# A two-layer graph network in one launch: earlier loads, later moments, denser products for the first group, and one copy moved from VectorE to ScalarE

## The chip, the cores and the metric

The kernel runs on one core of a Trainium2 chip, in float32 throughout. The metric is device time in microseconds (us) of one execution; lower is better. Engines are called PE (TensorE), DVE (VectorE), ACT (ScalarE), POOL (GpSimd) and SP (SyncE, which only issues DMAs here).

## What is computed

There are 64 graphs of 256 nodes with 256 features: `x` is 64 x 256 x 256 and `adj` has the same shape. Two layers follow, each with a normalization ahead of it and its input added back at the end:

```python
h = maximum(layernorm(x), 0)
A = adj + I;  d = rowsum(A) ** -0.5
x = x + relu((d A d) @ h @ W.T + b)               # layer 0
h = maximum(layernorm(x), 0)                       # layer 1 from here
conv = relu(bn2(conv17(relu(bn1(conv1(h))))) + h)  # 17 taps along the nodes
s = h @ w_se.T + b_se
msg = exp(-|s_i - s_j|^2) @ relu(h @ w_msg.T + b_msg)
x = x + GRU(input=[conv, msg], state=h)            # r, z, n gates
```

In the kernel the weight exp(...) is multiplied by the adjacency of the graph, transposed, as its mask.

## The kernel before

The work has two stages. **Stage 1** (lines 545 to 1280) walks over the graphs. One turn n of the loop at line 1190 works on several graphs at once, each at another step: `turn_h` of graph n-2, `aggregate` of graph n, `turn_cols` (even n), `turn_adj` of graph n+1, `pass_messages` of graph n-5, `messages` of n-2, `distance` (even n), `project` of n, `conv1` of n-2. After each group of matmuls stands `beat(us)`. **Stage 2** (from line 1282) computes the gates of the GRU for four groups of 16 graphs, and beside each group the convolution of the next one.

**Order of the work.** All instructions of PE, ACT, DVE and POOL keep the program's order (`Pinned`, line 94). Only the DMAs of SP are placed by the scheduler of the language, each as soon as it takes its buffer to be free and in program order among those that are ready; SP then runs them in that order. Follow-up work is put off by `after(k, go)` (line 247), which runs `go` at the (k+1)th beat from there. Within a turn there are nine beats and eight slots, `item()` (line 1154), into which extra work can be put.

**The convolution** with 17 taps is done in the frequency domain for 16 graphs at a time. `filter_part` (line 790) makes the spectra of the taps, in 32 steps. `spectrum` (line 294) transforms one half of a graph: 32 steps for a group, each of four matmuls into a tile `df` and a copy to `Xf` by ACT. `product` (line 328) multiplies one of 24 frequencies: matmuls into `y` and `y1`, a copy `k32` on ACT, two results on DVE (`Xf<-y,k`), one sum `xs` on POOL, three loads `wf` of 256 KB each. The inverse transform (`inverse_three`, `inverse_group`, `inverse_last`, lines 376 to 522) is cut into pieces of one instruction, on DVE, POOL and ACT. It starts when product u = 7 is done, and its last part when product 23 is.

**The planner of these pieces** is `Paced` (line 106). Pieces stand in lines, with a cost each (line 110: on DVE 0.15 us and 0.35 per 256 columns). A beat gives room, `share` times its length (0.31 on DVE, 0.5 on POOL, 0.25 on ACT in stage 1, line 1168), at most 1.0 saved up, and pieces are issued while there is room. `paced.lines` is empty before the inverse starts and after its last piece is issued. `paced.drain()` (line 1523) issues what is left when stage 2 begins.

**Pace of the slots.** For the first group, filter steps take the slots from turn 12 on, spectra from turn 29, then products. The rate is set by `FILTER`, `SPECTRA`, `PRODUCTS` (line 1188):

```python
pace[1] = min(pace[1] + pace[0], 1.0)
if items and pace[1] > 0.999:
    pace[1] -= 1.0
    items.pop(0)()
```

with `pace[0]` at `SPECTRA / 8`, later `PRODUCTS / 8`, and `pace[1]` at -3.0 when the spectra begin.

**Loads and moments of layer 0.** `load(g)` (line 816) brings x and adj of a pair of graphs, 512 KB each, into one of three buffers each. The buffer of x comes free when `rows` in `project` (line 935) has added x to the result; the same step stores that result, `x2d`. `row_moments` (line 832) takes mean and variance of the rows of x on DVE (four pairs of instructions for a pair of graphs), `degrees` (line 844) the row sums of adj, also on DVE; `factors` (line 862) on POOL makes scales of both, and `layer0_in` (line 876) on ACT the normalized input `hs` that `aggregate` reads.

**h2T.** `turn_h` (line 984) transposes the normalized input of layer 1 on PE into a PSUM tile `ht`. Its follow-up `keep` copies it into `h2T` in SBUF by DVE (line 997) and stores it (`hTd`). `messages` and `conv1` of the same turn multiply from h2T. It has two buffers, as have `x2`, `c1o` and `xnT`; h2T is written again when the store of two graphs before has landed.

**PSUM.** The tiles ht, ag, st, at, nm, di (four at once), o, df, y and y1 take turns in five banks, named `ps`.

**The hand-over.** When the loop ends, all pools of stage 1 but those of the convolution are closed and the pool `gates` is opened over their place. In it lie `wiT` and `whT` (weights, loaded at lines 1299 and 1300), `T1` to `T4` (sums of weights, made by POOL) and `xcT` (32 KB of each partition), the convolution's output, which `turn_outputs` (line 524) fills: PE transposes into `yt`, ACT and DVE copy out in turn.

Of the kernel before, what the change touches and what calls it, by code (L numbers as in the profile page):

```python
# [11 lines left out]
FP = mybir.dt.float32  # L12
# [16 lines left out]
OUT = 32  # L29
# [156 lines left out]
def gnn_kernel(  # L186
# [10 lines left out]
    B, N, D = x.shape  # L197
    P = 128
    KW = conv2_w.shape[2]
    NB = N // P  # L200
    DC = D // P
    G = 2
# [42 lines left out]
    paced = Paced(pool, vec, act)  # L245

    def after(beats, go):
        due.append([beats, go])
# [296 lines left out]
    with ExitStack() as one:  # L545
# [270 lines left out]
        def load(g):  # L816

            xt = io.tile([P, NR, D], FP, tag="x", name=f"x_{g}", bufs=3)
            at = io.tile([P, NR, N], FP, tag="adj", name=f"adj_{g}", bufs=3)
            st[g].update(both=(xt, at))  # L820
            for b in range(G):
                rb = slice(b * NB, (b + 1) * NB)
                st[g + b].update(xt=xt[:, rb, :], at=at[:, rb, :])
            if g > 0:
                nc.sync.dma_start(xt, x[g : g + G].rearrange("b (c p) d -> p (b c) d", p=P))
                nc.sync.dma_start(at, adj[g : g + G].rearrange("b (c p) d -> p (b c) d", p=P))
# [5 lines left out]
        def row_moments(g, rows):  # L832
            xt, _ = st[g]["both"]
            if "mv" not in st[g]:
                st[g]["mv"] = small.tile([P, NR, 2], FP, tag="mv0", name=f"mv0_{g}", bufs=1)
            for r in rows:
                s6 = small.tile([P, 6], FP, tag="st", name=f"st0_{g}_{r}")
                vec.bn_stats(s6, xt[:, r, :])
                vec.bn_aggr(st[g]["mv"][:, r, :], s6)
# [36 lines left out]
        def layer0_in(g, rows):  # L876

            xt, _ = st[g]["both"]
            rsd, nmr, dis = st[g]["rsd"], st[g]["nmr0"], st[g]["dis0"]
            if rows[0] == 0:  # L880
                hs = work.tile([P, NR, D], FP, tag="hs", name=f"hs_{g}")
                for b in range(G):
                    rb = slice(b * NB, (b + 1) * NB)
                    st[g + b].update(hs=hs[:, rb, :], dis=dis[:, rb])
            for r in rows:
                act.activation(
                    st[g + r // NB]["hs"][:, r % NB, :], xt[:, r, :], AF.Relu,
                    bias=nmr[:, r : r + 1], scale=rsd[:, r : r + 1],
                )
# [94 lines left out]
        def turn_h(g):  # L984
            s = st[g]
            t = bank(f"ht_{g}").rearrange("p (c i) -> p c i", c=DC)
            for dc in range(DC):
                for nb in range(NB):
                    pe.transpose(
                        t[:, dc, nb * P : (nb + 1) * P],  # L990
                        s["h2"][:, nb, dc * P : (dc + 1) * P],
                        ident,
                    )

            def keep():
                s["hT"] = work.tile([P, DC, N], FP, tag="h2T", name=f"h2T_{g}")
                vec.tensor_copy(s["hT"], t)
                nc.sync.dma_start(hT_d[g].rearrange("p (c n) -> p c n", c=DC), s["hT"])
            after(1, keep)

# [184 lines left out]
            items.append(products)  # L1185
            items.extend(lambda u=u: product(u) for u in range(1, UNITS))

        FILTER, SPECTRA, PRODUCTS = 2, 5, 3
        filtering = []
        for n in range(B + 5):  # L1190
            even, odd = n % G == 0, n % G == 1
            if filtering and not items:
                filtering.clear()
                while due:
                    beat(0.0)
                conv_start()
            if even and n + 2 * G < B:
                after(3, lambda n=n: load(n + 2 * G))
            if 2 <= n <= B + 1:
                turn_h(n - 2)  # L1200
            beat(0.4)
            item()
            if n < B:
                aggregate(n)
                if odd and n + 1 < B and n > 0:
                    after(2, lambda n=n: factors(n + 1))
                    for r in range(NR):
                        after((5, 7, 8, 9)[r], lambda r=r, n=n: layer0_in(n + 1, (r,)))
                if even and n + G < B:
                    after(4, lambda n=n: degrees(n + G))  # L1210
                if odd and n + 3 < B:
                    for r in (0, 2):
                        after(3 + r // 2, lambda r=r, n=n: row_moments(n + 3, (r, r + 1)))
            beat(1.7)
            item()
            if even and 4 <= n <= B + 2:
                turn_cols(n - 4)
            beat(0.2)
            if n + 1 < B:
                turn_adj(n + 1)  # L1220
            beat(0.4)
            item()
            if n >= 5:
                pass_messages(n - 5)
            beat(1.7)
            item(True)
            if 2 <= n <= B + 1:
                messages(n - 2)
            beat(1.7)
            item()  # L1230
            if even and 4 <= n <= B + 2:
                distance(n - 4)
            beat(0.6)
            item()
            if n < B:
                project(n)
            beat(1.7)
            item(True)
            if 2 <= n <= B:
                conv1(n - 2)  # L1240
            elif n == B + 2:
                conv1(B - 1)
            beat(1.7)
            item()
            if n == 0:
                small_turns()
                turn_part(wmT, nat_wm, 0, D, "wm")
                T(WI, 0)()
                L(WI, 4)()
                own_bank("ms", 0, bmB)  # L1250
            if n == 1:
                small_shift()
                turn_part(w1T, nat_w1, 0, D, "w1", scale=sc[:, 0:DC])
                beat(0.4)
                own_bank("c1", 0, b1B)
                T(WI, 2)()
                L(WH, 0)()
            if n >= 2 and later:
                for go in later.pop(0):
                    go()  # L1260
                if not later:
                    while due:
                        beat(0.0)
                    prep_stack.close()
                    spec_stack = ExitStack()
                    spec = spec_stack.enter_context(tc.tile_pool(name="spec", bufs=1))
                    tab = spec.tile([P, 3 * UNITS], FP, tag="tab", name="tab")
                    nc.sync.dma_start(tab, nc.inline_tensor(filter_table(), name="tab_c").ap())
                    tp = {k: filter_load(k) for k in range(2)}
                    filtering.append(True)  # L1270
                    pace[:] = FILTER / 2, -7.0
                    items.extend(
                        lambda k=k, j=j: filter_part(k, j) for k in range(4) for j in range(QC // 8)
                    )
# [19 lines left out]
    cv.beat = beat  # L1294
    cv.bank = lambda name: ps_m.tile([P, 2 * D], FP, tag="m", name=name)

    wiT = big.tile([P, 2 * DC, 3 * D], FP, tag="wiT", name="wiT")
    whT = big.tile([P, DC, 3 * D], FP, tag="whT", name="whT")
    nc.sync.dma_start(whT, wh_d)
# [220 lines left out]
    for q in range(1, GROUPS + 1):  # L1520
        share[:] = 0.6, 0.6, 0.3
        ld = gate_inputs(q - 1, 0)
        paced.drain()
        xcT = big.tile([P, DC, P, OUT], FP, tag="xcT", name=f"xcT_{q}")
        turn_outputs(xcT)
        for go in gate_parts(ld, xcT):
            go()
        todo = []
        if q < GROUPS:
            conv_begin(q)  # L1530
            for g in range(NG):
                if g >= NG - WF:
                    wf_load(g - NG + WF)
                for cb in range(DC):
                    spectrum(g, cb)
            for u in range(1, AHEAD):
                sums(u)
            todo = [lambda u=u: product(u) for u in range(UNITS)]
            for _ in range(LEAD):
                todo.pop(0)()  # L1540
        for g in range(NG):
            share[:] = (0.42, 0.55, 0.3) if todo else (0.51, 0.62, 0.3)
            between = [todo.pop(0) if todo else lambda: None for _ in range(PER)]
            ahead, nxt = None, None
            if g + 1 < NG:
                ahead = gate_inputs(q - 1, g + 1)
                nxt = gate_parts(ahead, xcT)
            gates(ld, between, nxt)
            ld = ahead
            if q + 1 < GROUPS and g >= NG - H1:  # L1550
                h1_load(q + 1, g - NG + H1)
# [34 lines left out]
```

## Time and profile before

| what | value |
|---|---|
| median of three runs | 2088.32 us (2087.17 to 2089.09) |
| the profiled execution | 2086.44 us |
| its span, first to last instruction | 2084.7 us |
| mean granted TensorE clock | 0.993 |
| busy, share of the span | PE 97%, weight load 83%, DVE 68%, ACT 47%, POOL 53% |
| stage 1, and the hand-over to it | 0 to about 848 us, then to 864 us |
| filter steps on PE | 161.8 to 364 us |
| spectra of the first group | until about 485 us |
| products of the first group | 485.7 to about 640 us |
| last transpose ht of stage 1 | 833.81 us |

Nearly all instructions carry line 102, the helper that records them, so groups are told apart by the names of the tiles: `ag<-adjH,hs` is the aggregation, `ms` the messages, `o` the projection, `c` the first convolution, `nm` the message passing. A number in brackets after an instruction is the time its engine stood idle before it, with what ended that. A turn of the loop can be found by its transposes `ht`, of which there is one group a turn from n = 2 on. Turns without slot work take about 9.5 us (odd n) and 10.8 us (even n) on PE; a turn with two filter steps takes 12.3 and 13.6, one with four spectra 12.8 and 14.1.

### The profile page before, as it was taken

How to read it: one execution, taken by the hardware profiler on the slowest of the kernel's cores; microseconds unless marked ns; L12 is line 12 of the kernel's file. 1: busy time of each engine (PE TensorE's matmuls, PEld its weight loads, DVE VectorE, ACT ScalarE, POOL GpSimd, SP SyncE). 2: the span in 40 equal slices, each digit the busy share in tenths (PEclk: the TensorE clock that was granted, in tenths of full speed). 3: DMA queues.
4: the chain of work that ended last, by engine and by line, in shares of the span. 5: the costliest groups of instructions: out<-in, count | busy, mean ns of one | idle time of the engine just before them, and what ended most of it. 6: DMA issues, size and time to landing. Idle time of an engine off the chain costs nothing. (4 is left out here: it accounts for less than half of the span.)

```text
span 2084.7 us, 31178 instructions
## 1 busy us (share of the span) xinstructions
PE 2029.4 (97%) x9977; PEld 1728.8 (83%) x9977; DVE 1413.3 (68%) x3207; ACT 987.4 (47%) x2139; POOL 1101.0 (53%) x1313
## 2 busy tenths in 40 slices
PE   7979999999999999899999999999999999999998
PEld 6867777888888878788888888888888888888887
DVE  6556666544498998426989814989923889965444
ACT  4756666665446666522334432334442234343333
POOL 4333333334675564447767617766725867644343
PEclk9989999999999999999999999999999999999999
DMA  8796888756765644556434356533356524322331
GB/s 306 241 243 224 236 255 271 228 171 205 237 220 193 199 167 147 197 175 214 128 103 128 117 176 197 172 107 122 114 150 203 160 86 127 118 87 90 93 100 61
DMA packets 292458, 352.85 MB, mean 169 GB/s; under 512 B 19492, under 2 KB 232119, under 8 KB 291639
## 3 DMA queue, kind: packets, MB, share of 16 engines
q1 hardware_dynamic: 291680, 346.26, 53.0%
q0 software_dynamic: 288, 4.46, 0.6%
q8 instruction: 80, 1.31, 0.3%
q14 instruction: 84, 0.68, 0.1%
q10 hardware_dynamic: 326, 0.14, 0.0%
HBM read 224.43 MB, written 126.35 MB: 168 GB/s over the span
## 5 line engine op out<-in xcount | busy, mean ns | idle before, releaser
L102 DVE TENSOR_TENSOR Xf<-y,k 128x256 f32<-128x256 f32 x184 | 69.1, 417 | 180.1 <-PE y L102 168.9
L102 DVE SCALAR_TENSOR_TENSOR Xf<-Xf 128x256 f32<-128x256 f32 (+1 forms) x248 | 183.2, 753 | 5.3 <-ACT Xf L102 4.2
L102 PE MATMUL ta<-T,S 128*128 128x256 f32 x768 | 186.6, 379 | 0.0
L102 PE MATMUL y<-wf,Xf 128*128 128x256 f32 x768 | 182.4, 380 | 1.7 <-DVE Xf L102 1.4
L102 POOL TENSOR_TENSOR rz<-u,p 128x256 f32<-128x256 f32 x64 | 47.8, 748 | 245.0 <-ACT u L102 245.0
L102 POOL TENSOR_TENSOR rs<-ve,mhalf 128x2 f32<-128x2 f32 (+1 forms) x65 | 46.9, 722 | 231.5 <-DVE nm L102 226.6
L102 ACT ACTIVATE rz<-rz 128x512 f32<-128x512 f32 x128 | 80.2, 627 | 180.1 <-DVE rz L102 180.1
L102 PEld LDWEIGHTS y<-wf,Xf 128*128 128x128 f32 x768 | 144.3, 190 | 24.5 <-DVE Xf L102 2.6
L102 PEld LDWEIGHTS ta<-T,S 128*128 128x128 f32 x768 | 145.9, 190 | 19.8
L102 PE MATMUL n<-wiT,hx 128*128 128x256 f32 x512 | 152.3, 379 | 0.0
L102 POOL TENSOR_TENSOR aT<-e,adjT 128x512 f32<-128x512 f32 x64 | 85.2, 1349 | 103.1 <-ACT e L102 103.0
L102 POOL TENSOR_TENSOR xs<-Xf 128x256 f32<-128x256 f32 x92 | 70.5, 772 | 130.9 <-ACT Xf L102 65.6
L102 PE MATMUL ag<-adjH,hs 128*128 128x256 f32 x512 | 123.4, 384 | 15.9 <-ACT hs L102 10.8
L102 DVE SCALAR_TENSOR_TENSOR h2l<-rz,h2l 128x256 f32<-128x256 f32 x128 | 102.8, 803 | 53.0 <-POOL h2l L102 53.0
L102 PE MATMUL o<-w0T,aggT 128*128 128x256 f32 x512 | 126.1, 390 | 6.4 <-ACT aggT L102 5.1
L102 PE MATMUL ms<-wmT,h2T 128*128 128x259 f32 x512 | 126.3, 389 | 6.0 <-DVE h2T L102 5.9
L102 PE MATMUL n<-whT,hx 128*128 128x256 f32 x512 | 131.4, 379 | 0.0
L102 PE MATMUL n<-wiT,xcT 128*128 128x256 f32 x512 | 131.4, 379 | 0.0
L102 PEld LDWEIGHTS ms<-wmT,h2T 128*128 128x128 f32 x512 | 95.9, 191 | 34.9 <-issue 13.5
L102 POOL TENSOR_TENSOR adjH<-adjT,eye 128x512 f32<-128x512 f32 x64 | 82.7, 1292 | 79.2 <-ACT adjT L102 79.1
L102 PE MATMUL c<-w1T,h2T 128*128 128x256 f32 x512 | 122.8, 383 | 0.0
L102 PE MATMUL nm<-aT,mso 128*128 128x256 f32 x512 | 121.7, 381 | 0.8 <-POOL aT L102 0.8
(182 smaller groups left out, 5251.9 us busy)
## 6 DMA issues: line engine op xcount, KB each, us to landing
wf<-wfd SPq DMA_DIRECT2D x284, 256.0 KB
wfd<-fo SPq DMA_DIRECT2D x32, 576.0 KB
x2d<-x SPq DMA_DIRECT2D x64, 256.0 KB
h2d<-h SPq DMA_DIRECT2D x64, 256.0 KB
hTd<-h2T SPq DMA_DIRECT2D x64, 256.0 KB
h1d<-c1o SPq DMA_DIRECT2D x64, 256.0 KB
xnd<-xnT SPq DMA_DIRECT2D x64, 256.0 KB
h1l<-h1d SPq DMA_DIRECT2D x64, 256.0 KB
```

The lines of the kernel that those rows point to most:

```text
L102: return self.tc.keep_in_program_order(getattr(self.engine, op)(*args, **kwargs))
```

## The change

Five edits are made together.

```diff
             def keep():
                 s["hT"] = work.tile([P, DC, N], FP, tag="h2T", name=f"h2T_{g}")
-                vec.tensor_copy(s["hT"], t)
+                (act.copy if any(paced.lines) else vec.tensor_copy)(s["hT"], t)
...
-        FILTER, SPECTRA, PRODUCTS = 2, 5, 3
+        FILTER, SPECTRA, PRODUCTS = 2, 7, 4
...
             if even and n + 2 * G < B:
-                after(3, lambda n=n: load(n + 2 * G))
+                load(n + 2 * G)
...
+                if even and 0 < n < B - G:
+                    for r in (0, 2):
+                        after(1 + r // 2, lambda r=r, n=n: row_moments(n + G, (r, r + 1)))
                 if even and n + G < B:
                     after(4, lambda n=n: degrees(n + G))
-                if odd and n + 3 < B:
-                    for r in (0, 2):
-                        after(3 + r // 2, lambda r=r, n=n: row_moments(n + 3, (r, r + 1)))
...
+    def outputs_turned(q):
+        return big.tile([P, DC, P, OUT], FP, tag="xcT", name=f"xcT_{q}")
+
+    xcT = outputs_turned(1)
     wiT = big.tile([P, 2 * DC, 3 * D], FP, tag="wiT", name="wiT")
...
         paced.drain()
-        xcT = big.tile([P, DC, P, OUT], FP, tag="xcT", name=f"xcT_{q}")
+        if q > 1:
+            xcT = outputs_turned(q)
         turn_outputs(xcT)
```

- **The copy h2T** is made by ACT while `paced.lines` holds pieces of an inverse, and by DVE otherwise.
- **SPECTRA** goes from 5 to 7 and **PRODUCTS** from 3 to 4.
- **The load** of a pair is written at the start of an even turn, where it stood three beats later.
- **The moments** of a pair were taken in the odd turn ahead of the even turn that takes its degrees; they are now taken in that even turn, two to three beats after `aggregate` and ahead of `degrees`.
- **xcT** of the first group is the first tile of its pool, so that it lies where `wiT` and `whT` lay, and these behind it. Later groups use the same place.

## The prediction

> **What bounds the kernel now.** I read, in this order, the shares of part 1, busy time by stretch of 25 us, the waits of each stretch, and the timelines of the stretches where TensorE (PE) is not full. Columns of the stretches: length, then busy us and instructions of PE, weight load, DVE, ACT and POOL, then the granted clock, DMA share and GB/s.
>
> ```profile
> 125.00:150.00 25.00, 15.41 (x82) 12.69 (x80) 8.24 (x30) 7.92 (x17) 6.99 (x9) 0.85 0.98 202
> 425.00:450.00 25.00, 25.00 (x133) 21.93 (x132) 11.00 (x37) 16.14 (x35) 7.76 (x10) 1.00 0.52 168
> 700.00:725.00 25.00, 23.09 (x122) 19.16 (x119) 23.57 (x64) 15.94 (x35) 15.58 (x18) 1.00 0.64 208
> 850.00:875.00 25.00, 20.23 (x120) 17.22 (x120) 12.01 (x18) 13.56 (x26) 13.12 (x18) 0.93 0.82 284
> ```
>
> PE is full nearly everywhere (425: 25.00 of 25), so work off PE is free there, and the end moves only where PE waits. Besides the start (10.9 us idle in the first 25) that is three places: one gap at 140, a string of small ones from 700 to 845 with DVE at 23.57 of 25, and the hand-over at 850. After 875 each 25 us has 23.9 to 25 us of PE; nothing there is edited.
>
> The gap at 140: the waits from 125 to 160, then PE, then SP's queue.
>
> ```profile
> DVE st L102 <- DMA x<-in_x_dram: 13.6, 1, 13.6
> PE ag L102 <- ACT hs L102: 10.2, 1, 10.2
> ...
> 150.60 2.93 PE L102 MATMUL ag<-adjH,hs 128*128 128x256 f32 x6 [10.18 <-ACT hs L102]
> 154.17 1.06 PE L102 MATMUL at<-ident,adj 128*128 128x128 f32 x4
> ...
> 131.22 0.39 SPq L945 DMA_DIRECT2D x2d<-x  x1
> 133.63 0.34 SPq L1026 DMA_DIRECT2D h1d<-c1o  x1
> 134.06 0.38 SPq L998 DMA_DIRECT2D hTd<-h2T  x1
> 135.74 0.39 SPq L825 DMA_DIRECT2D x<-in_x_dram  x1
> ```
>
> DVE stands 13.6 us before the moments of a pair whose x was issued at 135.74, behind the ten tp loads (119.5 to 129.3) and three stores. Behind DVE stand cols, behind those ACT's mso, behind that hs, which PE needs. PE then runs at half clock for a while (1.06 us where 0.60 is usual). `ht` to `ht`, this turn (n = 12) takes 139.38 to 164.85 = 25.5 us; turn 28, also even with one filter step, takes 358.58 to 370.75 = 12.2. **The gap costs 13.3 us.**
>
> The string: PE's waits from 640 to 910, and one case on DVE and PE.
>
> ```profile
> PE ms L102 <- DVE h2T L102: 5.9, 5, 2.1
> PE first L102 <- ACT xnT L102: 3.1, 1, 3.1
> PE yt L102 <- ACT xcT L102: 2.4, 1, 2.4
> ...
> 707.50 1.50 DVE L102 TENSOR_TENSOR Xf<-Xf,hr 128x256 f32<-128x256 f32 x1
> 708.92 0.68 DVE L102 COPY h2T<-ht 128x512 f32<-128x512 f32 x1
> ...
> 777.17 3.53 PE L102 MATMUL ms<-wmT,h2T 128*128 128x259 f32 x8 [2.07 <-DVE h2T L102]
> ```
>
> The largest item is h2T, late behind the inverse's pieces on DVE. The 2.07 us wait also dropped the clock (3.53 us for 1.9). The string's h2T part: 5.9 + 1.6 = 7.5 us.
>
> The hand-over:
>
> ```profile
> 850.94 0.56 ACT L102 COPY xnT<-nm 128x512 f32<-128x512 f32 x1
> 857.19 0.33 SPq L1299 DMA_DIRECT2D whT<-whd  x1
> 857.36 0.75 DVE L102 TENSOR_SCALAR xcT<-yt,sh 128x512 f32<-128x512 f32 x1 [3.20 <-DMA xnd<-xnT]
> ```
>
> PE ends the last nm at 848.44; its copy xnT comes at 850.94, since ACT waits 2.10 us for the inverse's last pieces; xnd is issued at 853.68; when it lands, at about 857.1 (3.4 us), the first xcT and whT start together. PE reaches the next spectra at 864.26.
>
> [...] the same 128x256 pieces take 0.42 us alone and 1.5 to 2.2 beside POOL. [...] The trace: 0.68 (h2T) and 0.58 (xnT).
>
> **The change, part by part.**
>
> *Loads sooner, moments later.* Each load is two SP transfers of 512 KB (31 of each in all), moved past h1d and hTd on SP. In steady state this gains nothing: x is issued at 434.66, 0.05 us after the x2d store whose rows free its buffer. In the crowd at 131 it passes two stores, about 2 us. The moments (4 x (0.40 + 0.18) = 2.3 us of DVE) move from the odd to the next even turn, some 8 us later for PE; so x, landed at 146.4 or sooner, holds DVE no more than a few us. Late next: x2d (issued at 131.22) and hTd (134.06), whose landing frees x2's and h2T's two buffers. Estimated from x's landing at 146.4 and 0.7 us per 256 KB at the 366 GB/s of 144 to 148: x2d lands at 143.6, h1d and hTd at about 145.8 and 146.5. PE then waits some 2.2 us for the bank under the next nm, 1.2 for h2T, and may lose 0.9 to the clock: 4.3 stays. **Gain 13.3 - 4.3 = 9 us** (2 to 13).
>
> *SPECTRA 5 to 7* changes no rate: `item` caps the pace at 1.0, so 0.625 and 0.875 both fire each second slot, 4 a turn. It only starts two slots earlier. *PRODUCTS 3 to 4* fires each second slot, not each third: 23 products take 46 slots, not 69. Products end 25 slots of 8 a turn sooner, in turn 43 instead of 46; the one that starts the inverse (u = 7) comes 9 slots sooner. Per product nothing changes (12 matmuls, k32, two DVE results of 0.42, one xs, three wf loads). Counted through the planner's rule (0.31 us of DVE cost per us of beat, 89.4 us of cost in all), the inverse now issues its last piece in turn 68, in the last beat but one; then in turn 67, about 12 us sooner. So ACT is free when the last nm ends: xnT at 849.0, xnd at 849.1, landed at 852.5, then the 7.1 us from first xcT to spectra as now: 859.7 for 864.26. **Gain 4.5 us** (2 to 6). The new place of xcT I cost at nothing: whT, the first T on POOL and xcT waited for one event though they lie in different places, so I read the wait as one on the whole old pool (in the gain's upper end if wrong). wf's DMA stays hidden: 4 x 0.77 MB in a turn of 10.2 + 4 x 2.6 = 20.6 us is 149 GB/s, beside about 70 of the graphs; 217 to 253 is moved there now.
>
> A product just ahead of `di` costs: at 502.28 PE waits 0.45 us, since `di` takes four of five banks. Every second slot puts one there in each even product turn, three of them: **loss 1.4 us** (0 to 5, when DVE is late with the product's results).
>
> *h2T on ACT* while the inverse has pieces (turns 39 to 67): 0.68 us off DVE, 0.58 onto ACT, which has 15.9 of 25 busy at 700, so about 17.4. Its hTd store is unchanged. Queued behind it on ACT are aggT and adjT; PE wants aggT 4 us after ag. h2T itself has 4.5 us from ht to ms. So the 7.5 us go. Late next: POOL's bursts slow DVE still, and moments, degrees and cols now stand together in the even turn. Now cols starts 1.3 us after ms ends in an even turn (700.73 against 699.4); behind it wait mso, the bank copy and e (0.6 + 0.6 + 0.3), then `di`'s bank, which PE wants 4.3 us after ms: 2.2 us of slack. The moments add 2.3, the copy takes 0.7 off, and the lightened odd turn starts DVE some 2 us earlier. So it should fit, with small misses: I leave 2.5. **Gain 5 us** (-12 to +9).
>
> Sum: 9 + 4.5 + 5 - 1.4 = 17 us off the span of 2084.7 (the profiled execution took 2086.44, 1.9 below the median of 2088.32). 2088.3 - 17 = **2071 us**.
>
> **Rivals.** *R1, DVE's bound moves, it doesn't go* (even turns and POOL bursts take back the 5 us): 9 + 4.5 - 1.4 = 12, 2076. For: DVE at 23.6 of 25. Against: POOL's bursts and DVE's heavy odd turns made the waits, and the odd turns get lighter.
> *R2, the early gap is the stores', not x's, and the hand-over is held elsewhere*: 2 + 1 + 3 - 1.4 = 5, 2083. For: SP and DMA are full at 130 (share 1.07). Against: the record names x.
> *R3, slower*: the even turn's DVE queue. If the odd turn's relief doesn't carry over, cols comes 1.3 + 1.6 = 2.9 us after ms; past the 2.2 of slack, 0.7 us of PE in each of 12 bare even turns (8.4), and in the four under a POOL burst 2 more and 1.7 of clock (14.8): 23 lost against 12 gained, 2099. For: e and mso sit behind cols in order. Against: DVE now starts even turns some 2.7 us behind and still keeps PE fed.
>
> **How the numbers follow.** Forecast 0.58 (own range 2063 to 2079), R1 0.20, R2 0.11, R3 0.11. A measurement here can tell about 0.2%, 4 us. Faster: 0.58 + 0.20 and a few hundredths of R2 = 0.81; same: the rest of R2, 0.08; slower 0.11. Range: 2062 (the early gap gone whole, the string gone whole) to 2085 (all of R2); outside lie R3 and a little below.
>
> **What would show it.** Right: no DVE wait for x over 5 us after 25; turn 12 under 18 us; no wait of PE for h2T on DVE; products 4 a turn, ended three turns earlier, spectra still 4 a turn; last nm to the next spectra 11 us, not 15.8. Wrong: PE waiting for e or mso's bank in even turns; for aggT behind a blocked ACT; a gap near 143 of over 5 us.

## The result and the profile after

| | before | after |
|---|---|---|
| median, five runs each | 2088.32 us (2087.17 to 2090.37) | 2079.37 us (2078.26 to 2080.93) |
| ratio to before | | 0.9957 (95%: 0.9942 to 0.9971) |
| span of the profiled execution | 2084.7 us | 2076.7 us |

The change makes the kernel 9 us faster, inside the range given, and half of the 17 us that were forecast. The time lies at the upper edge of the forecast's own 2063 to 2079, and nearest to R1's 2076. Where the 8 us between the two spans lie, from `ht` to `ht` in the timelines of PE (us; the forecast column is the prediction's own sum):

| stretch | before | after | gained | forecast |
|---|---|---|---|---|
| turn 12 (the early gap) | 25.5 | 17.3 | 8.1 | 9 |
| turns 13 to 28 | 205.9 | 205.7 | 0.2 | 0 |
| turns 29 to 46 (spectra, products) | 271.8 | 272.9 | -1.1 | -1.4 |
| turns 47 to 63 (no slot work) | 183.9 | 182.3 | 1.5 | 5 |
| turn 65 to the end of the last nm | 14.6 | 19.9 | -5.3 | 0 |
| last nm to the next spectra | 15.8 | 10.6 | 5.2 | 4.5 |
| from there to the end | 1220.4 | 1221.9 | -1.5 | 0 |

(The start up to turn 12 and turn 64 give 0.8 more. The last row is stage 2, which no edit touches; over all kernels below it lies between 1219.7 and 1224.0. Each row is one traced execution. From turn 13 to 63 a stretch repeats within 0.4 us in kernels whose edits don't touch it; turn 12 takes 16.9 to 18.7 us in the kernels with the moments moved.)

The stretches of 25 us of the kernel after, with the same columns as before (length, busy us and instructions of PE, weight load, DVE, ACT, POOL, then clock, DMA share, GB/s):

```profile
125.00:150.00 25.00, 22.04 (x118) 17.95 (x116) 12.02 (x39) 13.11 (x28) 8.38 (x12) 1.00 1.02 208
825.00:850.00 25.00, 18.32 (x93) 13.70 (x94) 12.14 (x19) 12.39 (x30) 10.83 (x10) 0.93 0.40 137
850.00:875.00 25.00, 24.02 (x134) 21.89 (x135) 6.54 (x9) 14.28 (x29) 10.99 (x15) 1.00 0.77 263
```

And of the kernel before, the one that the prediction doesn't show:

```profile
825.00:850.00 25.00, 21.59 (x112) 16.59 (x110) 19.17 (x41) 13.50 (x32) 9.78 (x10) 1.00 0.38 134
```

Compared with before: the stretch at 125 has 22.04 us of PE for 15.41, with DMA as full (share 1.02 for 0.98). The stretch at 850 is nearly full (24.02 for 20.23). But the one ahead of it, 825, has only 18.32 us for 21.59, and a clock of 0.93 for 1.00: a part of the idle time of the hand-over has moved ahead of the last nm.

**The early gap.** PE and, ahead of it, SP's queue in the kernel after:

```profile
143.72 1.99 PE L102 MATMUL nm<-aT,mso 128*128 128x256 f32 x8 [1.44 <-DVE pre L102]
147.23 2.02 PE L102 MATMUL ms<-wmT,h2T 128*128 128x259 f32 x8 [1.52 <-DVE h2T L102]
...
133.44 0.40 SPq L825 DMA_DIRECT2D x<-in_x_dram  x1
```

The wait of 10.18 us for hs is gone, and the load is issued at 133.44 for 135.74. What stays are the two waits that the prediction named as late next, for the bank under nm and for h2T: 1.44 and 1.52 us for the 2.2 and 1.2 worked out. DVE's waits for DMAs from 125 to 160 show that they are the stores' (us in total, times, longest), and none is for the load of x:

```profile
DVE x L102 <- DMA x2d<-x: 4.8, 1, 4.8
...
DVE h2T L102 <- DMA hTd<-h2T: 1.0, 1, 1.0
```

**The turns without slot work.** PE's waits from 655 to 835 us after (us in total, times, longest):

```profile
PE ag L102 <- POOL adjH L102: 2.8, 3, 1.4
PE ht L102 <- ACT e L102: 2.7, 2, 1.4
PE nm L102 <- DVE pre L102: 1.2, 1, 1.2
```

The 5.9 us for h2T by DVE are gone, as forecast. In their place PE waits for e, for adjH by POOL and for pre by DVE. The odd turns (nine, n = 47 to 63) take 85.5 us for 93.6 before, but the even ones (eight, 48 to 62) 96.8 for 90.3. Turn 56 shows how, on DVE, POOL, ACT and PE:

```profile
735.68 0.39 DVE L102 BATCH_NORM_STATS2 st<-x 128x6 f32<-128x256 f32 x1
...
736.98 1.21 DVE L102 TENSOR_REDUCE deg<-adj 128x4 f32<-128x1024 f32 x1
...
738.84 1.26 POOL L102 TENSOR_TENSOR hr<-hr,Xf 128x512 f32<-128x512 f32 x1
738.89 1.24 DVE L102 TENSOR_SCALAR pn<-deg 128x4 f32<-128x4 f32 x1
...
740.45 0.17 DVE L102 COPY cols<-ms 128x24 f32<-128x24 f32 x1
...
740.65 0.60 ACT L102 ACTIVATE mso<-ms 128x512 f32<-128x512 f32 x1 [2.95 <-DVE cols L102]
...
742.24 0.66 PE L102 MATMUL ht<-ident,h 128*128 128x128 f32 x4 [1.39 <-ACT e L102]
```

ms ends on PE at 736.5. DVE is then still at the moments (`st`), takes the degrees (`deg`) and pieces, and reaches cols, its copy of some columns of ms, only at 740.45, 3.9 us after ms. One of its small instructions, pn, takes 1.24 us for a median of 0.16, in the same time as POOL's `hr`. ACT stands 2.95 us before mso, e comes behind it, and the next ht waits for a bank that e has to empty. In the kernel before, cols came 1.1 us after ms in the same turn. The same wait of ht for e stands in turn 52 (cols 4.1 us after ms). It is the sign of being wrong that the prediction named first.

**The hand-over.** POOL, PE and ACT around the last nm of stage 1 in the kernel after:

```profile
835.77 1.48 POOL L102 TENSOR_TENSOR hr<-hr,Xf 128x512 f32<-128x512 f32 x1 [0.59 <-DMA hr<-h2d]
837.21 1.44 POOL L102 TENSOR_TENSOR aT<-e,adjT 128x512 f32<-128x512 f32 x1
...
839.48 1.45 POOL L102 TENSOR_TENSOR aT<-e,adjT 128x512 f32<-128x512 f32 x1
...
838.71 5.41 PE L102 MATMUL nm<-aT,mso 128*128 128x256 f32 x16 [3.48 <-POOL aT L102]
844.83 1.14 PE L102 MATMUL first<-brzB,ident 32*128 32x512 f32 x8 [0.72 <-ACT xnT L102]
...
847.65 1.26 ACT L102 ACTIVATE xcT<-yt,sh 128x512 f32<-128x512 f32 x2
```

POOL and PE at the same place in the kernel before:

```profile
843.39 2.68 POOL L102 TENSOR_TENSOR aT<-e,adjT 128x512 f32<-128x512 f32 x2 [7.29 <-ACT e L102]
846.44 0.73 POOL L102 TENSOR_TENSOR scr<-Xf,hr 128x256 f32<-128x256 f32 x1 [0.36 <-DVE Xf L102]
...
844.72 3.72 PE L102 MATMUL nm<-aT,mso 128*128 128x256 f32 x16 [0.28 <-POOL aT L102]
```

After the last nm all goes as forecast: `first`, the first matmuls of stage 2, waits 0.72 us for xnT and not 3.1, and xcT starts 3.5 us after nm's end. But the masks aT of graphs 62 and 63 now stand on POOL behind pieces of the inverse, which wait for DVE and for a load (`hr<-h2d`). PE waits 3.48 us for the first mask, and the two nm then take 5.41 us at a granted clock of 0.68, for 3.72 us at 1.00 before. In the kernel before, the same pieces stood behind both masks.

### The profile page after: what moved, and what is told of

Read it like the earlier page. It is cut to its first block, busy times and chain, and to the rows that moved or that the text cites. A ratio compares the mean times of both kernels' runs of the same rounds, so it can differ in the third digit from the quotient of the medians.

```text
span 2076.7 us, 31189 instructions
## 1 busy us (share of the span) xinstructions
PE 2028.5 (98%) x9977; PEld 1727.0 (83%) x9977; DVE 1404.7 (68%) x3181; ACT 997.5 (48%) x2165; POOL 1108.9 (53%) x1313
## 5 line engine op out<-in xcount | busy, mean ns | idle before, releaser
L102 PE MATMUL y<-wf,Xf 128*128 128x256 f32 x768 | 182.4, 380 | 2.5 <-DVE Xf L102 1.4
L102 POOL TENSOR_TENSOR rs<-ve,mhalf 128x2 f32<-128x2 f32 (+1 forms) x65 | 52.2, 803 | 226.8 <-DVE nm L102 221.6
L102 PEld LDWEIGHTS o<-w0T,aggT 128*128 128x128 f32 x512 | 95.3, 191 | 28.7 <-issue 5.6
```

Source lines behind the costliest of these rows:

```text
L102: return self.tc.keep_in_program_order(getattr(self.engine, op)(*args, **kwargs))
```

## The experiments

Theory at the start: the early gap was ended by the moments' move, not by the load's; moments in the even turn took the place of the h2T waits; the earlier tail of the inverse, a product of the denser slots, gives back ahead of the last nm what it gains behind it. All ratios are to the kernel before on the same chip, with 95% intervals. The stretches of all kernels stand in one table behind the third experiment.

**1. Loads and moments alone.** The kernel before, with these two edits of the change as they are in its diff:

```diff
-                after(3, lambda n=n: load(n + 2 * G))
+                load(n + 2 * G)
...
+                if even and 0 < n < B - G:
+                    for r in (0, 2):
+                        after(1 + r // 2, lambda r=r, n=n: row_moments(n + G, (r, r + 1)))
```

> The kernel before with two of the five edits: the loads of x and adj sooner, and the moments in the later, even turn. My theory: these two alone end the early gap, 8 us of the 9 that the change brings, and the products, spectra and h2T stay as they were: 2080 us, turn 12 at 17 us for 25.5. The rival, that the moments crowd the even turn for DVE when h2T is still copied there: the early gap goes as well, but 4 us or more come back as waits of PE for e, cols or h2T in turns 47 to 63, 2084 or above.

Measured: 2081.96 us, 0.9973 (0.9963 to 0.9983). Turn 12 takes 17.8 us, so the gap goes with these two edits. Turns 47 to 63 take 186.1 us, 2.3 more than before: some crowding, less than the rival's 4. **The two edits, one at a time:** moments alone, then load alone.

> The kernel before with one of the five edits: the moments in the later, even turn; loads where they were. My theory: DVE waited in the odd turn for an x that lands 14 us later; asked for only in the even turn, the same x is there in time, and the place of the load matters little: turn 12 at 17 to 18.5 us, as with both edits. The rival, that the load's earlier place ends the gap: turn 12 stays at 23 us or more.

> The kernel before with one of the five edits: the loads three beats sooner, moments where they were. My theory: x gains the two stores that it passes in SP's queue, some 2 us of the gap: turn 12 at 23.5 us, the rest unchanged, about 2085 to 2087. The rival, that the load alone ends the gap: turn 12 at 17 to 18 us, and 2079 to 2081, since no bare turn is crowded.

Measured: moments alone 2083.25 us, 0.9974 (0.9965 to 0.9984), turn 12 at 16.9 us; load alone 2087.05 us, 0.9998 (0.9990 to 1.0006), turn 12 at 23.7 us. DVE's wait for x in the odd turn, 13.6 us before, is still 12.0 us with the load alone, and gone with the moments alone. The load's place gives 1.8 us of the gap, and with the moments moved nothing more. So DVE's wait was ended by asking for x later, not by bringing it sooner.

**2. The copy alone.** The kernel before, with h2T by ACT:

```diff
-                vec.tensor_copy(s["hT"], t)
+                (act.copy if any(paced.lines) else vec.tensor_copy)(s["hT"], t)
```

> The kernel before with one of the five edits: h2T copied by ACT while the inverse has pieces. My theory: the copy alone brings the whole 7 us of turns 47 to 63 (177 us for 183.85), since moments stand in the odd turn here, and the other stretches stay: 2081. The rival, that the denser products have a part in those 7 us (the inverse is further on in the same turn): 180 us there, and 2084.

Measured: 2082.72 us, 0.9975 (0.9968 to 0.9983). Turns 47 to 63 take 177.1 us for 183.9: 6.8 us of the 7.5 at which the string of waits was counted. The denser products have no part in it. The kernel gains only 4.7 us, though: 2.3 of the 6.8 come back around the last nm (15.6 and 17.1 us for 14.6 and 15.8). The same is seen behind the last nm with loads and moments, with moments alone and with the load alone, 17.3 to 18.3 us. In all five kernels the first xcT by ACT starts 8.6 to 8.7 us after the last nm; but the 14 transposes yt that follow a wait there take 1.94 us before and 2.76 to 3.25 in the other four. With loads and moments the granted clock was 0.50 from 852.9 to 856.3, before 1.00 from 857.8 to 859.8. So the 2.2 us between 15.8 and 18.0 (loads and moments) lie behind the first xcT, where yt ran at the lower clock: ACT's waits for yt there come to 4.3 us, for 2.1 before. The wait ahead of the 14 transposes was about the same in both, 2.5 and 2.44 us; the trace of the kernel before is the better case.

**3. Copy and moments apart.** First the kernel after with loads and moments put back, then the kernel after with the copy put back to DVE.

> The kernel after with loads and moments put back where they were: denser spectra and products, h2T on ACT, the place of xcT. My theory (the moments in the even turn are what took the place of the h2T waits): the early gap is back, +8 us, but the bare turns 47 to 63 get 4 us faster than in the kernel after, since moments, degrees and cols no longer stand together: 2083.5. The rival, that the copy on ACT itself makes e late: the bare turns stay at 182 us, and the time is 2087.5, the early gap alone.

> The kernel after with h2T copied by DVE throughout. My theory: DVE, with moments, degrees and cols in the even turn and the copy too, is late for h2T again; the waits for h2T come back in turns 47 to 63, and 5 us are lost: 2084. The rival, that the copy on ACT brought nothing, since e is late behind it on ACT: 2079 or less, and the waits for e go.

Measured: 2081.30 us, 0.9968 (0.9955 to 0.9980), and 2081.53 us, 0.9976 (0.9966 to 0.9985). With the moments back in the odd turn the stretch 47 to 63 takes 176.8 us, with the copy back on DVE 184.9. So both edits meet in this stretch:

| turns 47 to 63, us | moments in odd turns | moments in even turns |
|---|---|---|
| h2T by DVE | 183.9 (before), 182.9 (load alone) | 186.1, 187.9, 184.9 |
| h2T by ACT | 177.1, 176.8, 176.8 | 182.3 (after), 182.1, 182.2, 182.4 |

With the moments in the odd turns the copy on ACT gives 7 us, with the moments in the even turns 2.6 (184.9 to 182.3): they take back 5.5 us of what the copy gives. All kernels, by stretch (us):

| kernel | turn 12 | 29 to 46 | 47 to 63 | 65 to last nm | last nm to spectra |
|---|---|---|---|---|---|
| before | 25.5 | 271.8 | 183.9 | 14.6 | 15.8 |
| after | 17.3 | 272.9 | 182.3 | 19.9 | 10.6 |
| loads and moments | 17.8 | 272.0 | 186.1 | 14.6 | 18.0 |
| moments alone | 16.9 | 272.0 | 187.9 | 14.6 | 17.3 |
| load alone | 23.7 | 271.8 | 182.9 | 14.6 | 18.3 |
| copy alone | 25.9 | 271.8 | 177.1 | 15.6 | 17.1 |
| after, loads and moments back | 25.4 | 272.5 | 176.8 | 19.9 | 10.6 |
| after, copy back on DVE | 17.2 | 273.4 | 184.9 | 19.5 | 10.6 |
| after, PRODUCTS 3 | 17.2 | 271.9 | 182.1 | 18.3 | 13.7 |
| after, xcT last | 17.6 | 272.9 | 182.2 | 20.0 | 10.6 |
| after, moments by phase | 17.6 | 272.6 | 176.8 | 21.0 | 10.6 |
| after, masks first | 18.0 | 272.9 | 182.4 | 15.0 | 17.2 |
| by phase, tail early | 18.7 | 273.0 | 181.1 | 16.5 | 10.7 |
| by phase, masks first | 17.1 | 272.6 | 176.8 | 15.1 | 18.0 |

**4. Moments by phase.** If the move helps only the early gap and harms only later turns, it should be made in the early turns alone. The kernel after, with

```diff
+        CUT = 38
...
-                if even and 0 < n < B - G:
+                if even and 0 < n < CUT:
...
+                if odd and CUT <= n + 1 and n + 3 < B:
+                    for r in (0, 2):
+                        after(3 + r // 2, lambda r=r, n=n: row_moments(n + 3, (r, r + 1)))
```

> The kernel after, with the moments in the even turn only up to turn 38 and in the odd turn from there. My theory: the early gap stays short (turn 12 at 17 us) and the bare turns 47 to 63 take 177 us, as in the run with loads and moments put back, instead of 182.3: 5 us off the kernel after, 2074. The rival, that the earlier loads (which stay) and not the moments crowd the bare turns: they stay at 182 us, and the time at 2079.

Measured: 2073.97 us, 0.9931 (0.9919 to 0.9943), the fastest of all medians here. Turn 12 stays at 17.6 us, the stretch 47 to 63 takes 176.8. PE's waits in this kernel from 655 to 835, for those shown of the kernel after:

```profile
PE nm L102 <- POOL aT L102: 4.5, 2, 3.5
PE ag L102 <- POOL adjH L102: 2.0, 2, 1.5
...
PE nm L102 <- DVE pre L102: 0.6, 1, 0.6
```

No wait of ht for e is left. In turns 52 and 56 cols comes 2.2 and 1.9 us after ms, for 4.1 and 3.9 in the kernel after: the 2 us between them are about the 2.3 us of the moments. These two turns get 3.0 us shorter; the rest of the 5.5 lies in turns 54, 58 and 62, where PE waits less for hs, adjH and pre. (The 3.5 us for aT is the one of the hand-over, which comes 5 us sooner here and so falls into the stretch.)

**5. The products' pace.** The kernel after with one number changed:

```diff
-        FILTER, SPECTRA, PRODUCTS = 2, 7, 4
+        FILTER, SPECTRA, PRODUCTS = 2, 7, 3
```

> The kernel after with PRODUCTS at 3 again (SPECTRA stays at 7). My theory: the denser products brought nothing, since their gain after the last nm (5.3 us) was given back just ahead of it, where POOL's last masks stand behind the tail of the inverse: 2079.5, with no wait for aT near 835 and the wait for xcT at 850 back. The rival, that the wait for aT comes of the copy on ACT or of the moments and would stand at 3 as well: then the 5 us after the last nm are lost and nothing is saved ahead of it, 2084.

Measured: 2078.37 us, 0.9958 (0.9946 to 0.9971), the same as after. The time is as I expected, one half of the reason is not: the wait for aT doesn't vanish (0.9 and 1.7 us at the last two nm), since here too the tail falls among the last masks, and the wait for xcT is back (2.7 us). Both stretches together take 32.0 us, for 30.6 after and 30.5 before. Turns 29 to 46 take 271.9 and not 272.9. So the denser products gain 1.4 us at the hand-over and lose 1 us in their own turns, which is nothing that the time shows.

**6. The place of xcT.** The kernel after, with the tile allocated where it was.

```diff
-    xcT = outputs_turned(1)
...
-        if q > 1:
-            xcT = outputs_turned(q)
+        xcT = outputs_turned(q)
```

> The kernel after, with xcT of the first group allocated where it was, behind the weights and sums of its pool. My theory: no difference, since whT, T and xcT all wait for one event of the whole old pool: 10.6 us from the last nm to the next spectra, 2079.4. The rival, that the new place let xcT or the weights start sooner and is a part of the 5 us gained there: 13 to 15 us, and 2082 to 2084.

Measured: 2078.83 us, 0.9960 (0.9947 to 0.9972), and 10.6 us from the last nm to the spectra in both. The place makes no difference.

**7. The masks ahead of the pieces.** The kernel after, with no room for pieces from turn 66 on, so that what is left is issued by `paced.drain()`:

```diff
         for n in range(B + 5):
             even, odd = n % G == 0, n % G == 1
+            if n == B + 2:
+                share[:] = 0.0, 0.0, 0.0
```

> The kernel after, with no piece of the inverse issued from the start of turn 66 on; what is left of them is issued when the loop has ended, behind the last masks and copies. My theory (the masks of graphs 62 and 63 stood on POOL behind pieces that wait for DVE and a load): the wait for aT near 835 goes, the last nm ends 4 to 5 us sooner; POOL's last pieces then end at about 843, and the transposes of Xf may wait 1 to 2 us for them, so 3 us are kept: 2076. The rival, that the tail of the inverse is what the hand-over waits for in any order: the wait moves to xnT, Xf or xcT, and the time stays at 2079.

Measured: 2079.96 us, 0.9962 (0.9949 to 0.9974). The wait for aT goes (15.0 us to the last nm's end), but 17.2 us follow it instead of 10.6. DVE and PE there:

```profile
843.63 0.76 DVE L102 SCALAR_TENSOR_TENSOR Xf<-Xf 128x256 f32<-128x256 f32 x2 [11.12 <-ACT Xf L102]
...
845.52 0.33 PE L102 MATMUL yt<-ident,Xf 128*128 128x128 f32 x1 [2.66 <-DVE Xf L102]
```

ACT's pieces are now issued behind the copies xnT, ta, tc and n; DVE stands 11.12 us before one of them, and PE's transposes yt wait for DVE. The rival holds in this order.

**8. Masks first, pieces right behind.** The kernel with moments by phase, and the last pieces issued at once behind the two masks:

```diff
-            after(4, lambda: mask(1))
+            after(2 if g + G == B else 4, lambda: mask(1))
+            if g + G == B:
+                after(2, lambda: share.__setitem__(slice(None), (1.0, 1.0, 1.0)))
...
+            if n == B + 2:
+                share[:] = 0.0, 0.0, 0.0
```

> The kernel with moments by phase, and with the masks of graphs 62 and 63 issued together ahead of the last six POOL pieces of the inverse; unlike in the run with all pieces held to the end, the pieces follow at once, ahead of the copies xnT of graphs 62 and 63 on ACT. My theory: there the hold failed because ACT's pieces stood behind seven copies and DVE waited 11 us for them; here they run at 836, the last pieces end at about 842, so the wait for aT goes (turn 65 to the last nm's end 15 to 16 us) and no more than 2 us come back after it: 2070.5. The rival, that the chain of the last pieces (10 us from POOL's scr on) is the hand-over's bound in any order: what the masks gain is lost after the last nm, 2074.

Measured: 2076.38 us, 0.9942 (0.9929 to 0.9955), not faster than moments by phase alone. The pieces end at 837.9, 4 us sooner than I expected, and still 18.0 us lie between the last nm and the spectra. SP's queue and ACT show why:

```profile
837.02 1.39 SPq L431 DMA_DIRECT2D hr<-h2d  x2
838.52 0.53 SPq L1116 DMA_DIRECT2D xnd<-xnT  x1
842.12 0.33 SPq L1312 DMA_DIRECT2D whT<-whd  x1
...
834.21 1.05 ACT L102 COPY xnT<-nm 128x512 f32<-128x512 f32 x2
...
842.07 1.27 ACT L102 ACTIVATE xcT<-yt,sh 128x512 f32<-128x512 f32 x2 [3.88 <-DMA xnd<-xnT]
```

The last xnT is copied at 835.3. Its store xnd stands in SP's queue behind two loads of `hr`, and those wait until POOL has emptied a buffer (for its `Xf`, the inverse's tail). So xnd goes at 838.52, lands at 842.1, and only then xcT and whT start. This was a part of the hand-over in the kernel before too: xnT was done there at 851.5, a load of `hr` was issued at 853.04, xnd at 853.68, 2.2 us after its data was ready. Slower transposes are a part of the 18.0 us again: behind a wait of 4.07 us the 14 yt take 3.25 us, in the kernel with moments by phase alone 1.94.

**9. The tail wholly ahead.** The kernel with moments by phase and a larger share of DVE, so that the last pieces stand ahead of the masks of graph 60:

```diff
-            share[:] = 0.31, 0.5, 0.25
+            share[:] = 0.35, 0.5, 0.25
```

> The kernel with moments by phase (even turn to 38, odd from there), and DVE's share of a beat for pieces of the inverse at 0.35 instead of 0.31, so that its last pieces stand ahead of the masks of graph 60 and not among those of 62 and 63. My theory: the wait for aT at the last nm goes (turn 65 to the end of the last nm 15 us instead of 20 to 21) and the 10.6 us after it stay, so this time both are had; one to two us may be lost to a denser DVE in turns 39 to 63: 2070. The rival, that the tail only meets other masks (aT of 58 to 61) and DVE's other work, and takes back in turns 58 to 64 what it gives at the end: 2074 to 2077.

Measured: 2076.35 us, 0.9949 (0.9936 to 0.9961). The hand-over takes 16.5 and 10.7 us, 4.4 less than by phase alone, nearly what was expected; the last nm waits 0.27 us for aT, the one of graph 60 still 2.4. But turns 47 to 63 take 181.1 for 176.8, and it is all lost. The two longest of PE's waits there:

```profile
732.61 2.00 PE L102 MATMUL ag<-adjH,hs 128*128 128x256 f32 x8 [1.20 <-POOL adjH L102]
...
778.84 1.99 PE L102 MATMUL nm<-aT,mso 128*128 128x256 f32 x8 [1.22 <-DVE pre L102]
```

One is for POOL, one for DVE. DVE is later there: cols comes 1.1 to 2.9 us after ms in the even turns 48 to 60, in the kernel without the larger share 0.0 to 2.2. The rival holds: what is gained at the end is lost ahead of it, though in turns 50 to 60 and more by waits for adjH and pre than for the masks that it named.

## Why the prediction was right and where it was wrong

**The early gap** was right in place, mechanism and size: forecast 9, measured 8.1. Moments and not the load end it (experiment 1), the load alone is worth about 2 us, and what is late next is what the prediction named. That PE might lose 0.9 us to the clock there was an estimate; after waits of 1.44 and 1.52 us none was lost (granted clock 1.00 from 143.72 to 150).

**The pace of the slots** came as counted: 4 spectra and 4 products a turn, the products over in turn 43. The loss in these turns is 1 us, for 1.4, but not as it was counted: two waits of 0.45 us stand ahead of `di`, in turns 38 and 40, and the one in turn 38 was there before. So that place costs 0.45 us more, and the rest lies in small waits from turn 42 to 46.

**h2T on ACT** is the first failed term, "so it should fit, with small misses: I leave 2.5", a gain of 5. The waits for h2T did go, and the copy alone brings 6.8 us of the 7.5. What fell is the step behind it, that moments and cols fit into the even turn since "the lightened odd turn starts DVE some 2 us earlier". The miss is 5.5 us, for the 2.5 left. Its clearest part is the mechanism of R3, in its place: cols comes 4.1 and 3.9 us after ms in turns 52 and 56, past the slack of 2.2. In turn 56 that is 2.8 us later than before, more than the 2.3 us of the moments, though the copy's 0.7 is gone: nothing is left of the relief of 2 us. Why it is not there was not followed, but for one thing that the turn shows: a small instruction of DVE that takes as long as POOL's beside it (pn 1.24 us, `hr` 1.26). R3's price was far off, though, 23 us in 12 turns; it decides in two of the eight even turns, for 3.0 us. As a cost it is R1's: DVE's bound moves and takes back the 5 us. One edit was priced for the gap at 140 and taken to fit in all later turns, while it should have been priced in each phase.

**The hand-over** is the second failed term. Its own sum was right (4.5 forecast, 5.2 measured; xcT's place costs nothing, as assumed), in part without its reason: it let xnd follow xnT at once, which saves the 2.2 us of experiment 8, and didn't say that a load ahead of xnd in SP's queue had cost them. Left out was what the tail of the inverse passes when it moves 12 us ahead: the masks of graphs 62 and 63 on POOL. That wait (3.48 us) and the lower clock behind it (1.7) make up 5.2 of the 5.3 us, so the net is zero. (Against the other kernels with the old pace, 17.1 to 18.3 us from nm to spectra, the two stretches together are 1.4 to 2.3 us shorter; experiment 2 has the reason.) The tail also came less far ahead than counted: POOL's last piece ends 17.6 us after ht of turn 65, for 20.9 before. The prediction asked what is free once the tail is gone, and not what stands behind the tail where it goes. That PE would wait for aT was in neither the forecast nor a rival; R2, with 1 us for the hand-over, came nearest there.

**One reading of the trace** was wrong and bore on no term: of DVE's pieces of 128x256 beside POOL, the 2.2 us were the time of two (2.17 and 2.22 us, x2). One took about 1.5 us at most.

The sum with the measured terms: 8.1 + 0.2 - 1.1 + 1.5 - 5.3 + 5.2 + 0.8 (start and turn 64) - 1.5 (stage 2) = 7.9 us between the spans.

What stays open: whether the 5 us at the last nm can be had at all. Three orders were tried (experiments 7 to 9). Each freed the last masks and lost about as much elsewhere: by ACT's order, by SP's, by DVE and POOL in earlier turns. An order that frees POOL, ACT and SP at once was not tried. SPECTRA at 7 was not measured apart from the rest; the traces show 4 spectra a turn with 5 and with 7.

## What to carry to other kernels

When work in an in-order queue is moved ahead, list for each queue that it uses, SP's too, what stood ahead of it and now stands behind it; the gain where it was is only half of the sum. A move that cures a wait in one phase of a loop should be priced in each other phase and, where it costs there, made for that phase alone: here a condition on the turn was worth 5.4 us more than the change itself. Where the transfers are full, as here (DMA share 0.98 and 1.02 from 125 to 150), a later consumer can cure a wait for a load better than an earlier issue: 8.5 us for 1.8 here.

## What the runs showed of the hardware

TensorE's clock dropped after a wait of 3.48 us (16 matmul steps of nm in 5.41 us at a granted clock of 0.68, for 3.72 us at 1.00) and did not after 1.44 and 1.52 us (1.00 from 143.72 to 150). The kernel before shows a drop after 2.07 us (ms in 3.53 us at 0.55, for 1.91 us elsewhere) and none after 2.44 us (the 14 yt of experiment 2 in 1.94 us at 1.00). In experiment 9 a wait of 2.39 us brought none either (8 steps of nm in 1.99 us). So in these traces the length of a wait alone doesn't tell.

An instruction of DVE on four columns took 1.24 us for a median of 0.16 (pn, turn 56 of the kernel after), while POOL worked on 128x512 from 738.84 to 740.10. In the kernel before, `sq<-cols` on six columns took 1.18 us from 734.35, for a median of 0.17, beside POOL's `adjH` of 1.26 us from 734.24, and `pn<-deg` 0.70 us from 699.71, for a median of 0.16, beside POOL's `Xf` of 0.73 us from 699.65. In these three cases a small instruction of DVE lasted about as long as the large one beside it on POOL.
